# Every other expert's rows: transposed by VectorE from gathered quarters instead of by TensorE

## The chip, the cores and the metric

The kernel runs on one core of a Trainium2 chip. The metric is the device time of one execution in microseconds (us); a time given for a kernel is the median of several runs.

## What is computed

One transformer block: attention over 2048 tokens of width 512, then a mixture of 64 experts (each token goes to 4 of them) plus two shared experts. All data are float32. What matters here is the routed part of the second half:

```python
flat = x.reshape(N, Dx)                    # N = 2048 tokens, Dx = 512
scores = softmax(flat @ Wr + router_bias)  # E = 64 experts
topk_scores, topk_idx = top_k(scores, 4)
...
xb = zeros((E, CAP, Dx)).at[eid, pos].set(flat[tok], mode='drop')   # CAP = 128 seats an expert
h = silu(einsum('ecd,edh->ech', xb, Wg)) * einsum('ecd,edh->ech', xb, Wu)
yb = einsum('ech,ehd->ecd', h, Wd)
y = yb[eid, minimum(pos, CAP - 1)] * (w * valid)[:, None]
out = zeros((N, Dx)).at[tok].add(y)        # and the shared experts are added
```

## The kernel before

The kernel has four stages one after the other, and in each the order of the instructions on every engine is written out by hand.

**Attention** (to about 1772 us from the span's start) goes over heads; its probabilities are brought into 32x32 blocks by DMAs and turned by VectorE (`turn_blocks`, L461).

**Routing and output projection** (1772 to 1968): for each of 16 tiles of 128 tokens, TensorE multiplies the attention outputs by `wo` (L917). The outputs of two tiles (a pair) come from DRAM by `load_ab` (L544) on SP's queue, into one of two buffers `v`. VectorE normalises the tile (`norm`, L728) into `h`, and GpSimd's queue writes `h` to the DRAM tensor `h2d` (L743). TensorE transposes `h` into `h2T` (`turn_h`), computes router logits, and VectorE chooses experts (`choose`, `positions`). `seat_tokens` (L852) adds up, on TensorE, a table of which token sits on which seat of which expert; for the last block VectorE turns the table into token numbers `tok` (128 seats x 64 experts, L869).

**Experts** (2005 to 2371). The steps of expert e are

- `load_xb(e)` (L1190): an indirect DMA on GpSimd's queue gathers the expert's 128 rows of 512 numbers from `h2d` into `xb` (three buffers);
- `expert_turn(e)` (L1199): four 128x128 transposes on TensorE into PSUM (`tpx`, L1202), one copy by ScalarE into `xbT` (L1204);
- `expert_up(e)` (L1206): four matmuls into `pse`, of which there is one PSUM buffer (tag `pl`, `bufs=1`); then `glu`: a sigmoid on ScalarE (L968) and two products on VectorE (L969, L970), of which the last writes `he` and so frees `pse`;
- `expert_mid(e)` (L1222): one transpose `tph` and a copy;
- `expert_down(e)` (L1228): the matmul `psy` (L1230), its product `y` with the gate on VectorE (L1232), and the write to the DRAM tensor `ybd` from ScalarE's queue.

`expert_step(e)` lists, with a cost each, the turn of e+1 (and the gather for e+3), the up of e, the mid of e-1 and the down of e-2. `merge` (L83) lays this list and the list of the shared experts' work beside each other: it always takes the next entry of the list of which the smaller share of cost is done. The shared experts' work comes as units of "pst" products (`first` to `fourth`, L1064; `second` has three additions and three sums of weights on VectorE) and as chains of eight matmuls "psd" (L1126).

**Tail** (from 2371): GpSimd gathers four rows of `ybd` per token (`gather`, L1258), VectorE adds them up, and the last shared work runs on TensorE.

Of the kernel before, what the change touches and what calls it, by code (L numbers as in the profile page):

```python
# [9 lines left out]
F32 = mybir.dt.float32  # L10
BF16 = mybir.dt.bfloat16
U32 = mybir.dt.uint32
AF = mybir.ActivationFunctionType
ALU = mybir.AluOpType
# [4 lines left out]
P = 128  # L19
# [4 lines left out]
def adaln_block_kernel(  # L24
# [23 lines left out]
    nc = tc.nc  # L48
    _, N, D = x.shape
    H, _, DH = Q_w.shape  # L50
    E, _, HE = Wg.shape
    S, _, HS = Sg.shape
    K = 4
    CAP = 128
    NT = N // P
    DC = D // P
# [9 lines left out]
    dram = ctx.enter_context(tc.tile_pool(name="dram", bufs=1, space=DRAM))  # L66

    ident = const.tile([P, P], F32)
# [9 lines left out]
    gb = const.tile([P, D], F32)  # L78
    atd = dram.tile([H, DH, N], F32)
    h2d = dram.tile([N, D], F32)  # L80
    ybd = dram.tile([E * CAP, D], F32)

    def merge(streams, marks):  # L83
# [40 lines left out]
    with ExitStack() as att:  # L124
# [63 lines left out]
        with tc.tile_pool(name="pre", bufs=1) as pre, tc.manual_schedule():  # L188
# [4 lines left out]
            for b in range(NB):  # L193
                xb = pre.tile([P, 4, D], F32, name="xb", bufs=NB)
                nc.sync.dma_start(
                    out=xb, in_=x[0, b * 512 : (b + 1) * 512, :].rearrange("(i p) d -> p i d", p=P)
                )
                xs.append(xb)
                if b == 0:
                    wms = {}  # L200
                    for i in (1, 0):
                        wms[i] = pre.tile([P, DC, D], F32, name="wm", bufs=2)
                        nc.sync.dma_start(
                            out=wms[i],
                            in_=wmod[:, i * D : (i + 1) * D].rearrange("(k p) n -> p k n", p=P),
# [343 lines left out]
        xts = {}  # L549
# [52 lines left out]
        with tc.manual_schedule():  # L602
# [9 lines left out]
            for n, (hd, s) in enumerate(steps):  # L612
# [12 lines left out]
                if hd == H - 1 and s == 0:  # L625
# [4 lines left out]
                    for i in range(0, H, 4):  # L630
                        nc.gpsimd.dma_start(
                            out=wo[:, i : i + 4, :], in_=O_w[i : i + 4].rearrange("h p d -> p h d")
# [39 lines left out]
    keep = ctx.enter_context(tc.tile_pool(name="keep", bufs=1))  # L672
# [8 lines left out]
    psO = ctx.enter_context(tc.tile_pool(name="psO", bufs=2, space=PSUM))  # L681
# [5 lines left out]
    rt = rts.enter_context(tc.tile_pool(name="rt", bufs=1))  # L687
# [4 lines left out]
    iota = rt.tile([P, E], F32)  # L692
    places = rt.tile([P, CAP], F32)
    own = rt.tile([P, 1], F32)
    tok = keep.tile([CAP, E], U32)
    hs_ = {}
    mvs = {}
    logits = {}
# [5 lines left out]
    def route_consts():  # L704
        nc.sync.dma_start(out=wr, in_=Wr.rearrange("(k p) e -> p k e", p=P))
        nc.sync.dma_start(out=rb, in_=router_bias.partition_broadcast(P))
        make_upper_triangular(nc, before, val=1.0, diag=False)
        nc.gpsimd.memset(onesb, 1.0)
        nc.gpsimd.iota(
            iota, pattern=[[1, E]], base=0, channel_multiplier=0,  # L710
            allow_small_or_imprecise_dtypes=True,
        )
        nc.gpsimd.iota(
            places, pattern=[[1, CAP]], base=0, channel_multiplier=0,
            allow_small_or_imprecise_dtypes=True,
        )
        nc.gpsimd.iota(
            own, pattern=[[0, 1]], base=0, channel_multiplier=1,
            allow_small_or_imprecise_dtypes=True,
        )  # L720

    def load_x(j):
        nc.sync.dma_start(
            out=acc[:, 4 * j : 4 * j + 4, :],
            in_=x[0, j * 512 : (j + 1) * 512, :].rearrange("(i p) d -> p i d", p=P),
        )

    def norm(t):  # L728

        st = rt.tile([P, 6], F32, name="st", bufs=3)  # L730
        nc.vector.bn_stats(st, acc[:, t, :])
        mv = rt.tile([P, 2], F32, name="mv", bufs=3)
        nc.vector.bn_aggr(mv, st)
        rstd = rt.tile([P, 1], F32, name="rstd", bufs=3)
        nc.scalar.activation(rstd, mv[:, 1:2], AF.Sqrt, bias=eps, scale=1.0)
        nc.vector.reciprocal(rstd, rstd)
        h = rt.tile([P, D], F32, name="h", bufs=4)
        nc.vector.tensor_scalar(
            h, acc[:, t, :], mv[:, 0:1], rstd, ALU.subtract, ALU.mult
        )  # L740
        nc.vector.tensor_mul(h, h, cb)
        nc.vector.tensor_add(h, h, sb)
        nc.gpsimd.dma_start(out=h2d[t * P : (t + 1) * P, :], in_=h)  # L743
        hs_[t] = h

    def turn_h(t):
# [105 lines left out]
    def seat_tokens(b):  # L852


        t0, nt = BLOCKS[b]
        seat, who = seats.pop(b)
        for n in range(nt * K):
            i, k = divmod(n, K)
            nc.tensor.matmul(
                out=table,  # L860
                lhsT=seat[:, n, :],
                rhs=who[:, i, k].rearrange("p j e -> p (j e)"),
                start=(b == 0 and n == 0),
                stop=(b == len(BLOCKS) - 1 and n == nt * K - 1),
            )
        if b == len(BLOCKS) - 1:
            tb = rt.tile([CAP, 2 * E], F32, name="tb")
            nc.vector.tensor_copy(tb, table)
            nc.vector.scalar_tensor_tensor(  # L869
                tok, tb[:, E:], float(P), tb[:, :E], ALU.mult, ALU.add  # L870
            )

    table = psO.tile([CAP, 2 * E], F32, name="table", tag="tr")
    ALL = ((0, 4), (4, 8), (8, 12), (12, 16))
# [12 lines left out]
    with tc.manual_schedule():  # L887
# [6 lines left out]
        for t in range(NE):  # L894
            ps = psO.tile([P, D], F32, name="pso", tag="y")
            nc.tensor.matmul(
                out=ps,
                lhsT=last3[:, t * P : (t + 1) * P] if t < NE - 1 else ones,
                rhs=wo[:, H - 1, :],
                start=True,  # L900
                stop=True,
# [4 lines left out]
        for t in range(NE, NT):  # L906
# [3 lines left out]
            if i == 1 and pr >= NP - 1 - S:  # L910
                s = pr - (NP - 1 - S)
# [3 lines left out]
            ps = psO.tile([P, D], F32, name="pso", tag="y")  # L915
            for hd in range(H):
                nc.tensor.matmul(  # L917
                    out=ps,
                    lhsT=abs_[pr][:, hd, i * P : (i + 1) * P],
                    rhs=wo[:, hd, :],  # L920
                    start=(hd == 0),
                    stop=(hd == H - 1),
# [20 lines left out]
    with ExitStack() as ex:  # L943
# [11 lines left out]
        def load_up(e):  # L955
            w = ewp.tile([P, DC, 2, HE], F32, name="wgu")
            nc.sync.dma_start(out=w[:, :, 0, :], in_=Wg[e].rearrange("(k p) h -> p k h", p=P))
            nc.sync.dma_start(out=w[:, :, 1, :], in_=Wu[e].rearrange("(k p) h -> p k h", p=P))
            weights[e] = w
# [5 lines left out]
        def glu(dst, pg, pu, width):  # L965

            sig = sgp.tile([P, width], F32, name=f"sig{width}")
            nc.scalar.activation(sig, pg, AF.Sigmoid)  # L968
            nc.vector.tensor_mul(sig, sig, pg)  # L969
            nc.vector.tensor_mul(dst, sig, pu)  # L970
# [213 lines left out]
        xbp = wts.enter_context(tc.tile_pool(name="xbp", bufs=2))  # L1184
        xbs = {}
        xts = {}
        ups = {}
        hts = {}

        def load_xb(e):  # L1190
            xbs[e] = xbp.tile([CAP, D], F32, name="xb", bufs=3)
            nc.gpsimd.indirect_dma_start(  # L1192
                out=xbs[e][:, :],
                out_offset=None,
                in_=h2d[:, :],
                in_offset=bass.IndirectOffsetOnAxis(ap=tok[:, e : e + 1], axis=0),
            )

        def expert_turn(e):  # L1199
            tp = psO.tile([P, DC, P], F32, name="tpx", tag="tr")  # L1200
            for k in range(DC):
                nc.tensor.transpose(tp[:, k, :], xbs[e][:, k * P : (k + 1) * P], ident)  # L1202
            xts[e] = xbp.tile([P, DC, CAP], F32, name="xbT")
            nc.scalar.copy(xts[e], tp)  # L1204

        def expert_up(e):  # L1206
            ps = psO.tile([P, 2 * HE], F32, name="pse", tag="pl", bufs=1)
            for k in range(DC):
                nc.tensor.matmul(  # L1209
                    out=ps,  # L1210
                    lhsT=xts[e][:, k, :],
                    rhs=weights[e][:, k].rearrange("p i h -> p (i h)"),
                    start=(k == 0),
                    stop=(k == DC - 1),
                )
            if e + 3 < E:
                load_up(e + 3)
            he = xbp.tile([CAP, HE], F32, name="he")
            glu(he, ps[:, :HE], ps[:, HE:], HE)
            ups[e] = he  # L1220
# [7 lines left out]
        def expert_down(e):  # L1228
            ps = psO.tile([CAP, D], F32, name="psy", tag="y")
            nc.tensor.matmul(out=ps, lhsT=hts[e], rhs=downs[e], start=True, stop=True)  # L1230
            y = xbp.tile([CAP, D], F32, name="y")
            nc.vector.tensor_mul(y, ps, gb)  # L1232
            nc.scalar.dma_start(out=ybd[e * CAP : (e + 1) * CAP, :], in_=y)

        def expert_step(e):
            out = []

            def turn():
                if e + 3 < E:
                    load_xb(e + 3)  # L1240
                expert_turn(e + 1)

            def down():
                expert_down(e - 2)
                if e + 1 < E:
                    load_down(e + 1)

            if e + 1 < E:
                out.append((512, turn))
            if e < E:  # L1250
                out.append((1024, lambda: expert_up(e)))
            if 0 <= e - 1 < E:
                out.append((128, lambda: expert_mid(e - 1)))
            if e >= 2:
                out.append((512, down))
            return out
# [34 lines left out]
        with tc.manual_schedule():  # L1291
# [13 lines left out]
            for n, (_, f) in enumerate(tail):  # L1305
                f()
                upto = min(NT, READY[n])
                while done < upto:
                    t = order[done]
# [37 lines left out]
```

## Time and profile before

| | |
|---|---|
| median of 3 runs | 2510.37 us (2509.43 to 2513.41) |
| the profiled execution | 2493.62 us, its span 2491.8 us |
| mean granted TensorE clock | 0.994 of full speed |
| TensorE busy | 2419.3 us, 97% of the span |
| VectorE busy | 1514.8 us, 61% |
| DMA traffic | 326.25 MB in 224399 packets |
| transposes `tpx` (L1202) | 256, mean 273 ns |
| copies `xbT` (L1204) | 64, mean 585 ns |
| gathers `xb` (L1192) | 64, mean 1012 ns on GpSimd's queue |
| GpSimd's queue in the expert stage | waits 269.8 us in 58 waits for TensorE's `tpx` |

PE is TensorE, PEld its loading of weights, DVE VectorE, ACT ScalarE, POOL GpSimd, SP the queue that only issues DMAs; a small q (SPq, ACTq) marks an engine's DMA issues. Matmuls overlap on TensorE, so the duration of one is longer than the distance from its start to the next one's. A row of a group gives: line, engine, operation, what it writes and reads, count, then total busy time and mean of one in ns, then how long the engine was idle before them and what ended that. A row of the timeline gives start, length, engine, line and operation; brackets hold the idle time before it.

### The profile page before, as it was taken

Reading aid. Unit: us, or ns where it says so; the run is one execution under the profiler, and the core shown is the slowest. Engines: PE = TensorE matmul, PEld = TensorE weight load, DVE = VectorE, ACT = ScalarE, POOL = GpSimd, SP = SyncE. Lnnn points to the kernel's source line nnn. Section 1 sums busy time; section 2 is a strip of 40 time slices with the busy share of each in tenths; the row PEclk is TensorE's granted clock in tenths of the full one; section 3 lists DMA queues with packets and bytes.
Section 4 is the critical chain, followed back from the end, with each engine's and each line's share of the span. In section 5 each row is a group of like instructions: output and inputs, shape, how many; then the busy total and the mean of one; then the engine's idle time right before and its main releaser. Section 6 shows DMA issues by size and latency. Waiting matters only on the chain.

```text
span 2491.8 us, 26256 instructions
## 1 busy us (share of the span) xinstructions
PE 2419.3 (97%) x8525; PEld 1526.6 (61%) x8525; DVE 1514.8 (61%) x2966; ACT 656.0 (26%) x1476; POOL 249.2 (10%) x314
## 2 busy tenths in 40 slices
PE   7999999999999999999999999979999999999999
PEld 4666666666666666666666666545554476876844
DVE  4566666666666666666666666565465572553664
ACT  3233233332333323333233333221111221222200
POOL 0000000000000000000000000041000021111164
PEclk9999999999999999999999999989999999999999
DMA  4234434444344443444444444475524266878665
GB/s 140 62 91 107 116 95 110 107 103 109 90 121 102 97 120 94 112 111 103 109 97 121 104 101 108 109 227 135 164 81 152 89 180 209 250 213 251 198 191 161
DMA packets 224399, 326.25 MB, mean 131 GB/s; under 512 B 32100, under 2 KB 140680, under 8 KB 224264
## 3 DMA queue, kind: packets, MB, share of 16 engines
q1 hardware_dynamic: 195656, 246.96, 38.4%
q0 software_dynamic: 19392, 60.84, 8.1%
q10 hardware_dynamic: 9216, 16.78, 1.8%
q8 instruction: 69, 1.13, 0.2%
q14 instruction: 66, 0.54, 0.1%
HBM read 139.91 MB, written 41.94 MB: 73 GB/s over the span
## 4 chain that ended last, share of the span: by engine, by line
PE 67%; DVE 17%; SPq 6%; DMA 4%; issue 4%; ACT 1%; DVEq 0%; POOL 0%; ACTq 0%; POOLq 0%
PE pqk L169 12%; PE ps L408 12%; PE po L479 9%; DVE pt L461 7%; PE pso L917 6%; SPq L451 6%; PE pv L329 5%; PE pst L1064 5%; PE pse L1209 4%; PE psd L1126 4%; DVE nm L421 4%; DMA pt<-p 3%; PE psg L980 3%; DVE p L397 3%; PE psy L1230 2%
## 5 line engine op out<-in xcount | busy, mean ns | idle before, releaser
L427 ACT ACTIVATE p<-ps,nm 128x1024 f32<-128x1024 f32 (+7 forms) x384 | 331.9, 864 | 1040.5 <-DVE nm L425 368.4
L408 PE MATMUL ps<-kt,qt 128*128 128x512 f32 (+3 forms) x1280 | 535.2, 535 | 43.0 <-ACT p L427 42.1
L479 PE MATMUL po<-pt,v 128*128 128x256 f32 (+1 forms) x2304 | 567.5, 369 | 7.0 <-DVE pt L461 3.6
L479 PEld LDWEIGHTS po<-pt,v 128*128 128x128 f32 x2304 | 426.4, 191 | 220.3 <-issue 155.8
L421 DVE TENSOR_REDUCE nm<-ps 128x1 f32<-128x1024 f32 (+7 forms) x384 | 349.6, 910 | 91.1 <-PE ps L408 82.4
L461 DVE STREAM_TRANSPOSE pt<-pt 128x1664 f32<-128x1664 f32 (+2 forms) x160 | 318.0, 1988 | 64.2 <-DMA pt<-p 59.9
L408 PEld LDWEIGHTS ps<-kt,qt 128*128 128x128 f32 x1280 | 235.5, 191 | 193.3 <-issue 126.9
L420 DVE TENSOR_TENSOR ps<-ps,causal 128x128 f32<-128x128 f32 x256 | 74.4, 291 | 349.9 <-PE ps L408 349.9
L489 POOL DMA_DIRECT2D atd<-at x128 | 78.2, 612 | 1650.0 <-ACT at L488 1625.4
L329 PE MATMUL pv<-wv,hT 128*128 128x256 f32 x1024 | 240.4, 379 | 0.0
L169 PE MATMUL pqk<-hT,wk 128*128 128x512 f32 x512 | 232.7, 598 | 0.0
L169 PE MATMUL pqk<-hT,wq 128*128 128x512 f32 x512 | 231.4, 596 | 0.0
L397 DVE TENSOR_SCALAR p<-p,rs 128x1024 f32<-128x1024 f32 (+7 forms) x384 | 221.7, 606 | 9.3 <-DMA p<-atd 0.2
L329 PEld LDWEIGHTS pv<-wv,hT 128*128 128x128 f32 x1024 | 195.0, 190 | 31.0 <-issue 1.9
L917 PE MATMUL pso<-hT,v 128*128 128x512 f32 x384 | 173.7, 598 | 0.0
L169 PEld LDWEIGHTS pqk<-hT,wk 128*128 128x128 f32 x512 | 98.3, 193 | 102.9 <-issue 100.5
L169 PEld LDWEIGHTS pqk<-hT,wq 128*128 128x128 f32 x512 | 98.1, 192 | 97.1 <-issue 93.9
L1209 PE MATMUL pse<-wgu,xbT 128*128 128x256 f32 x512 | 121.1, 380 | 0.0
L917 PEld LDWEIGHTS pso<-hT,v 128*128 128x128 f32 x384 | 69.7, 191 | 71.4 <-issue 70.4
L1126 PE MATMUL psd<-wsd,hs 128*128 128x512 f32 x256 | 111.5, 593 | 0.0
L1209 PEld LDWEIGHTS pse<-wgu,xbT 128*128 128x128 f32 x512 | 93.9, 191 | 11.6 <-issue 1.0
L1192 POOL DMA_INDIRECT xb<-h2d,tok x64 | 64.8, 1012 | 300.8 <-PE tpx L1202 269.8
(264 smaller groups left out, 1943.3 us busy)
## 6 DMA issues: line engine op xcount, KB each, us to landing
pt<-p SPq DMA_DIRECT2D x768, 104.0 KB, 2.2
pt<-p SPq DMA_DIRECT2D x256, 124.0 KB, 2.3
pt<-p SPq DMA_DIRECT2D x256, 108.0 KB, 2.2
atd<-at POOLq DMA_DIRECT2D x128, 128.0 KB, 2.3
wgu<-in_L_ffn_Wg_dram SPq DMA_DIRECT2D x64, 256.0 KB, 4.3
wgu<-in_L_ffn_Wu_dram SPq DMA_DIRECT2D x64, 256.0 KB, 4.7
wd<-in_L_ffn_Wd_dram SPq DMA_DIRECT2D x64, 256.0 KB, 3.9
ybd<-y ACTq DMA_DIRECT2D x64, 256.0 KB, 3.7
```

Of the source, the lines that this page charges most:

```text
L169: nc.tensor.matmul(out=ps, lhsT=w[:, k, :], rhs=hT[:, k, j * 512 : (j + 1) * 512], start=(k == 0), stop=(k == DC - 1),)
L329: nc.tensor.matmul(out=ps, lhsT=hT[:, k, t * P : (t + 1) * P], rhs=wv[:, k].rearrange("p i d -> p (i d)"), start=(k == 0), stop=(k == DC - 1),
L397: nc.vector.tensor_scalar(cols[:, :, a:b], cols[:, :, a:b], rs[:, n : n + 1], None, ALU.mult)
L408: nc.tensor.matmul(out=ps[:, o : o + wo], lhsT=q, rhs=kts[hd, (c0 + o) // 512][:, :wo], start=True, stop=True,)
L421: nc.vector.tensor_reduce(nm[:, n : n + 1], ps[:, :w], AX.X, ALU.max, negate=True)
L427: nc.scalar.activation(rows[:, r0 + c0 // P : r0 + (c0 + w) // P], ps[:, :w].rearrange("q (r b k) -> q r b k", b=4, k=32), AF.Exp, bias=nm ...
L451: nc.sync.dma_start(out=pt[32 * b : 32 * (b + 1), a * w : (a + 1) * w], in_=pb[32 * a : 32 * (a + 1), b * w : (b + 1) * w],)
L461: nc.vector.transpose(part, part)
L479: nc.tensor.matmul(out=po if wide else po[:, P:], lhsT=vts[g][:, kt, hh * DH : (hh + 1) * DH], rhs=rows[:, r : r + last + 1 : last] if wid ...
L917: nc.tensor.matmul(out=ps, lhsT=abs_[pr][:, hd, i * P : (i + 1) * P], rhs=wo[:, hd, :], start=(hd == 0), stop=(hd == H - 1),)
L1126: nc.tensor.matmul(out=ps, lhsT=hsh[b, f][:, i * P : (i + 1) * P], rhs=wsd[:, f, :], start=(f == 0), stop=(f == NHC - 1),)
L1209: nc.tensor.matmul(out=ps, lhsT=xts[e][:, k, :], rhs=weights[e][:, k].rearrange("p i h -> p (i h)"), start=(k == 0), stop=(k == DC - 1),)
```

## The change

- `norm` also writes each tile of `h`, in four DMAs on SP's queue, to a second DRAM tensor `h2q`. There a token's row is four quarters of 128 numbers; quarter b holds columns 32b to 32b+31 of each of the four chunks of 128 columns.
- After the last seats, four small matmuls with slices of the identity (`pick`, made by GpSimd in `route_consts`) spread the token numbers so that partition 32a+r has, for b = 0 to 3, the token of seat 32b+r; VectorE makes 4 x token + a of it (`tokq`).
- For odd experts `load_xb` gathers with four indirect DMAs of 128 rows of 128 numbers from `h2q`. The tile then consists of 32x32 blocks that already lie in the block that they belong to after a transpose.
- For odd experts `expert_turn` is one VectorE instruction that transposes the sixteen 32x32 blocks of each group of 32 partitions, straight into `xbT`; TensorE's four transposes and ScalarE's copy remain for even experts.
- In `expert_step` the turn of an odd expert counts 0 in place of 512, which shifts how `merge` lays the two lists beside each other.

```diff
+    h2q = dram.tile([N, D], F32)
...
+    quarter = rt.tile([P, 1], F32)
+    pick = rt.tile([P, 4, 4, 32], F32)
     tok = keep.tile([CAP, E], U32)
+    tokq = keep.tile([P, 4, E], U32)
...
+        for b in range(4):
+            nc.gpsimd.memset(quarter[32 * b : 32 * (b + 1), :], float(b))
+            nc.gpsimd.tensor_copy(pick[:, :, b, :], ident.rearrange("p (t r) -> p t r", r=32))
...
         nc.gpsimd.dma_start(out=h2d[t * P : (t + 1) * P, :], in_=h)
+        for b in range(4):
+            nc.sync.dma_start(
+                out=h2q[t * P : (t + 1) * P, b * P : (b + 1) * P].rearrange(
+                    "p (k d) -> p k d", d=32
+                ),
+                in_=h.rearrange("p (k b d) -> p b k d", b=4, d=32)[:, b],
+            )
...
             nc.vector.scalar_tensor_tensor(
-                tok, tb[:, E:], float(P), tb[:, :E], ALU.mult, ALU.add
+                tb[:, :E], tb[:, E:], float(P), tb[:, :E], ALU.mult, ALU.add
             )
+            nc.vector.tensor_copy(tok, tb[:, :E])
+            ps = psO.tile([P, 4, E], F32, name="psq", tag="tr")
+            for b in range(4):
+                nc.tensor.matmul(
+                    out=ps[:, b, :],
+                    lhsT=pick[:, b].rearrange("p a r -> p (a r)"),
+                    rhs=tb[:, :E],
+                    start=True,
+                    stop=True,
+                )
+            nc.vector.tensor_scalar(tokq, ps, 4.0, quarter, ALU.mult, ALU.add)
...
         def load_xb(e):
...
+            else:
+                xbs[e] = xbp.tile([P, D], F32, name="xb", bufs=3)
+                for b in range(4):
+                    nc.gpsimd.indirect_dma_start(
+                        out=xbs[e][:, b * P : (b + 1) * P],
+                        out_offset=None,
+                        in_=h2q.rearrange("n (b f) -> (n b) f", b=4),
+                        in_offset=bass.IndirectOffsetOnAxis(ap=tokq[:, b, e : e + 1], axis=0),
+                    )
...
         def expert_turn(e):
...
+            else:
+                xt = xbp.tile([P, DC, CAP], F32, name="xbT")
+                nc.vector.transpose(
+                    xt.rearrange("p k (b s) -> p b k s", s=32),
+                    xbs[e].rearrange("p (b k s) -> p b k s", b=4, s=32),
+                )
+                xts[e] = [xt[:, k, :] for k in range(DC)]
...
             if e + 1 < E:
-                out.append((512, turn))
+                out.append((512 if e % 2 == 1 else 0, turn))
```

More of the change, by code (lines that the diff above doesn't have):

```diff
@@ L1190, in load_xb @@
         def load_xb(e):
[L1191 to L1197, printed above, removed]
-        def expert_turn(e):
[L1200 to L1204, printed above, removed]
+            if e % 2 == 0:
+                xbs[e] = xbp.tile([CAP, D], F32, name="xb", bufs=3)
+                nc.gpsimd.indirect_dma_start(
+                    out=xbs[e][:, :],
+                    out_offset=None,
+                    in_=h2d[:, :],
+                    in_offset=bass.IndirectOffsetOnAxis(ap=tok[:, e : e + 1], axis=0),
+                )
+            else:
+                xbs[e] = xbp.tile([P, D], F32, name="xb", bufs=3)
+                for b in range(4):
+                    nc.gpsimd.indirect_dma_start(
+                        out=xbs[e][:, b * P : (b + 1) * P],
+                        out_offset=None,
+                        in_=h2q.rearrange("n (b f) -> (n b) f", b=4),
+                        in_offset=bass.IndirectOffsetOnAxis(ap=tokq[:, b, e : e + 1], axis=0),
+                    )
+        def expert_turn(e):
+            if e % 2 == 0:
+                tp = psO.tile([P, DC, P], F32, name="tpx", tag="tr")
+                for k in range(DC):
+                    nc.tensor.transpose(tp[:, k, :], xbs[e][:, k * P : (k + 1) * P], ident)
+                xt = xbp.tile([P, DC, CAP], F32, name="xbT")
+                nc.scalar.copy(xt, tp)
+                xts[e] = [xt[:, k, :] for k in range(DC)]
+            else:
+                xt = xbp.tile([P, DC, CAP], F32, name="xbT")
+                nc.vector.transpose(
+                    xt.rearrange("p k (b s) -> p b k s", s=32),
+                    xbs[e].rearrange("p (b k s) -> p b k s", b=4, s=32),
+                )
+                xts[e] = [xt[:, k, :] for k in range(DC)]
         def expert_up(e):
@@ L1210, in expert_up @@
                     out=ps,
-                    lhsT=xts[e][:, k, :],
+                    lhsT=xts[e][k],
                     rhs=weights[e][:, k].rearrange("p i h -> p (i h)"),
```

## The prediction

> **What bounds the kernel now.** The first view is the busy table with the 40 slices: TensorE is busy 97% of the span and nine tenths or more in all slices but two. VectorE, second, is at 61%.
>
> ```profile
> PE 2419.3 (97%) x8525; PEld 1526.6 (61%) x8525; DVE 1514.8 (61%) x2966; ACT 656.0 (26%) x1476; POOL 249.2 (10%) x314
> ...
> PE   7999999999999999999999999979999999999999
> ```
>
> Second, the same by stretches: the routing stage (1805 to 1968 us from the span's start), the whole expert stage (2005 to 2371), and inside it a part with "pst" units (2125 to 2230) and one with "psd" chains (2060 to 2125). The columns are engine busy times, clock, DMA share and GB/s.
>
> ```profile
> 2125.00:2230.00 105.00, 105.00 (x495) 85.06 (x495) 66.74 (x162) 27.00 (x71) 20.80 (x19) 1.00 0.81 240
> 2060.00:2125.00 65.00, 65.00 (x245) 40.58 (x244) 17.99 (x41) 12.60 (x36) 10.39 (x11) 1.00 0.72 217
> 2005.00:2371.00 366.00, 366.00 (x1599) 272.39 (x1598) 189.00 (x448) 84.00 (x228) 61.70 (x62) 1.00 0.74 222
> 1805.00:1968.00 163.00, 162.69 (x560) 81.64 (x559) 95.27 (x266) 23.96 (x37) 5.40 (x10) 1.00 0.27 94
> ```
>
> TensorE is full through all 366 us of the expert stage, at the full granted clock; VectorE is 52% busy there (64% among units), GpSimd 17%, the DMA engines 74%. Third, the list of waits from 2006 us on, TensorE's own rows: one wait of 0.7 us. So here TensorE's work sets the end, and a microsecond taken from its queue is a microsecond, as long as nothing new makes it wait.
>
> **What is removed.** 32 of 64 `expert_turn` lose four transposes on TensorE and a PSUM copy on ScalarE. Two rows by form give durations, and the timeline of one step gives what a step costs:
>
> ```profile
> L1202 PE MATMUL tpx<-ident,xb 128*128 128x128 f32 x256 | 38.2, 273 | 0.0
> L1204 ACT COPY xbT<-tpx 128x512 f32<-128x512 f32 x64 | 37.3, 585 | 145.9 <-DVE y L1232 58.0 <-PE tpx L1202 33.9 <-PE pse L1209 22.2
> ```
>
> ```profile
> 2086.75 0.60 PE L1202 MATMUL tpx<-ident,xb 128*128 128x128 f32 x4
> ...
> 2087.18 1.89 PE L1209 MATMUL pse<-wgu,xbT 128*128 128x256 f32 x8
> ...
> 2088.91 0.27 PE L1224 MATMUL tph<-ident,he 128*128 128x128 f32 x1
> ...
> 2089.02 1.02 PE L1230 MATMUL psy<-wd,heT 128*128 128x512 f32 x2
> 2089.11 0.28 ACT L968 ACTIVATE sig<-pse 128x128 f32<-128x128 f32 x1 [0.43 <-PE pse L1209]
> ...
> 2089.75 0.29 DVE L970 TENSOR_TENSOR he<-sig,pse 128x128 f32<-128x128 f32 x1
> ...
> 2089.88 0.60 PE L1202 MATMUL tpx<-ident,xb 128*128 128x128 f32 x4
> ```
>
> Read starts, not durations: the transposes overlap, and from the first one's start to the next matmul's is 2087.18 - 2086.75 = 0.43 us (0.44 a step later). So 32 x 0.435 = **13.9 us** leave TensorE's queue. The ScalarE copies (32 x 0.585) lie beside it and bring nothing. "TensorE: Matmul & The Clock Gate", Part 4, in the Trainium skill, gives a transpose about 275 ns in a kernel, which agrees with the mean of 273 ns here; as a price it would make 128 x 0.275 = 35 us, an estimate from that page. The spacing of the starts decides against it.
>
> **What is added, beside other work.**
> (a) VectorE: 32 block transposes, 128x512. Line L461 has three widths: 1664 in 1.907 us, 1984 in 2.238, so 1.03 ns a column and 0.19 fixed: 0.72 us each, 23 us in 366. The nearest rows bound it: a 128x512 scalar pass takes 0.547 (L738), the 1664 form 1.91; the four-dimensional pattern is not in the trace, and I take 0.72. Units then go from 64% to about 70%. I charge 0.5 us of new waits; the range keeps 0 to 6.
> (b) GpSimd: an odd expert needs four gathers. An unblocked gather starts every 1.25 us (2002.71, 2004.13 at the stage's start: 1.42), so a pair of experts costs 5 x 1.3 = 6.5 us of the 11.1 that it lasts (355 us / 64 x 2). `load_xb(e+3)` is released by the turn of e and needed at the turn of e+3, three steps on, at least 14.6 us in the new order. Four gathers take 3 x 1.3 to the last start, and 4.8 us (median of xb's landing, 8.4 at most) to land: 8.7, or 12.3 at worst. Cost nothing; without that cover VectorE stands in its queue, and the sigmoid products behind it hold `pse`.
> (c) SP: 64 writes to `h2q`, four a tile, 512 pieces of 128 bytes each; nearest `wr`, 512 pieces of 256 bytes, issued in 0.44 us and landed in 7.2 behind other loads. SP waits for `h` of the tile; what is queued behind are the next pair's `load_ab` (L544) and the shared weights. `h` of the last tile of a pair is ready 7 to 8 us after the pair's last matmul (h2d issues at 1814.79 and 1846.97; pairs end at 1807.5 and 1839), four issues take 2.4, the loads 2 and land in 5.2: 18 us into a pair that lasts 31.7. So 13 us of slack; TensorE waits for nothing. The DMA engines are 27% busy there. Last, `wgu` now follows tile 15's writes: 1979 in place of 1969, ten us of issue, landed by about 1995, wanted after 2008. Cost 0, kept 0 to 4. "DMA: Bandwidth & Descriptors", Specifications, speaks against this edit: pieces under 512 bytes cost a read-modify-write. If that doubled these writes, the 13 us would still hold them; no row here shows 128-byte pieces.
> (d) `pick` and `quarter`, eight small GpSimd operations after 1773.3, ahead of the first h2d write at 1780.5 (0.16 to 0.3 us are rows like them). They hide.
>
> **What is added on the path.**
> (e) The four `psq` matmuls stand in TensorE's queue right after the seat table and need `tb`. Now `tb` is written 1999.77 to 2000.05, the token indices end at 2000.32, and TensorE went on at 1999.41. Hand-over 0.2, then four 128x64 products of two passes (L758: eight starts in 0.84): TensorE goes on at 2001.4. **+2.0 us** (1.5 to 2.5).
> (f) In the new order the first `pse` follows expert 0's transposes at once; before, expert 1's and two products stood between. The copy is exposed: transposes at 2012.39, copy at 2013.08 for 0.58, 0.2 to hand over, less the 0.43 of the transposes: **+1.0** (0.8 to 1.3).
> (g) Expert 2's gather waits behind expert 1's four: POOL starts at about 2002.4, expert 2's gather at 2009, landing near 2013.7; TensorE wants it at 2013.4. **+0.5** (0 to 3).
> (h) `pse` has one buffer. In the step above, `pse` ends at 2088.91 and is free at 2090.04 (end of `he`), plus 0.2: 1.33 us. Between two `pse` stand tph 0.11, psy 0.87 and the transposes 0.43: 1.41, just enough. An odd step with nothing of the shared expert in it now has 0.98: wait 0.35. The changed order has eight such steps (11, 13, 17, 19, 41, 43, 45, 49): **+2.8** (0 to 3.5).
>
> **Sum:** -13.9 + 2.0 + 1.0 + 0.5 + 2.8 + 0.5 = **-7.1 us**. The profiled execution took 2493.62 (span 2491.8); it would be 2486.5. It lies 16.8 us under the median of the runs, 2510.37; nothing in the trace says where that is, and I take the step off the median: **2503.3**. What follows the expert stage (gathers of `ybd`, psd chains) begins from its last expert and moves up whole. A difference of 0.2%, 5 us, is about what a measurement of this kernel tells from none.
>
> **Rivals.**
> 1. *The covers are better than I charge*: (h) and (a) vanish, -13.9 + 3.5 = -10.4, 2500. For: at (h) TensorE has waited for nothing so far. Against: the arithmetic of one `pse` buffer. Chance 0.15.
> 2. *VectorE's queue takes it back.* The transposes stand ahead of the sigmoid products; among units VectorE also has 2.5 us of sums in one piece. Were each odd step late by 0.3 us, 32 x 0.3 = 9.6 more: +2, 2513; at half of that -2, 2508. For: in-order queue, 70%. Against: no TensorE wait for VectorE beyond 0.7 us today, and the tight steps hold few sums. Chance 0.25, about no change.
> 3. *Slower: the four gathers come too late.* Place: `load_xb` on POOL in the short stretches. It decides once issue and landing exceed 14.6 us: with 1.3 a gather the landing must pass 10.7 us (8.4 is the longest now), or a gather must cost 2.2 us in place of 1.3, so that five fill a pair. At 1 us late per odd expert: -7 + 32 = +25, 2535; at half, +9, 2519. For: DMA already at 81% among units, and the quarters are four times as many pieces of a quarter the size. Against: the bytes are the same, and the weights already come in 512-byte rows at 4.3 to 4.7 us. Chance 0.2, the routing stage's delays (c) included.
> 4. *It does not do what it says*: half the transposes still on TensorE. The order of instructions shows 32 groups of four in place of 64, so no weight.
>
> **Numbers.** Forecast 0.40 (2499 to 2507), rival 1 0.15, rival 2 0.25 (2506 to 2514), rival 3 0.20 (2515 and up, half of it under 2521). The range 2496 to 2520 leaves out the upper half of rival 3 and a little below. Faster by over 0.2%: 0.55; within: 0.25; slower: 0.20.
>
> **What would show it.** Right: the expert stage some 10 us shorter and TensorE still full; 128 tpx in place of 256; a stop of 1 us before psq and of 0.35 us before `pse` in the eight steps, ended by `he`; L1249 near 0.72 us; no TensorE wait on `v`. Wrong: VectorE idle before L1249 until a DMA of `xb` in many steps (rival 3), `pse` held by a late `sig` (rival 2), or TensorE waiting for `v<-atd` in the routing stage.

## The result, and the profile after

In the first comparison the changed kernel took 2509.65 us (2504.44 to 2516.13, 12 runs), the kernel before 2510.51 (2508.22 to 2513.75, 12 runs): ratio 0.9995, 95% interval 0.9986 to 1.0004. That is no difference that can be measured; the forecast was 7.1 us less. The profiled execution took 2504.44 us (span 2502.4), where 2486.5 was worked out.

One thing has to be said ahead of the rest. The later runs came to several chips, and these are of two sorts: on some the kernel before takes about 2497 us, on the others about 2510. The first comparison was made where it takes 2510; the profile of before that the prediction stands on (2493.62) has the time of the 2497 sort; like all profiles of that sort it holds landing times of gathers, which no profile of the 2510 sort does. Below, "a 2497 chip" and "a 2510 chip" mean just that, and every ratio is against runs of before on the same chip.

The page of the changed kernel, then the stretches of the prediction (columns: busy time of TensorE, weight load, VectorE, ScalarE and GpSimd, clock, DMA share, GB/s):

```profile
PE 2414.9 (97%) x8405; PEld 1514.2 (61%) x8405; DVE 1534.0 (61%) x3000; ACT 637.0 (25%) x1443; POOL 342.9 (14%) x418
...
PE   7999999999999999999999999979999989999989
```

```profile
1805.00:1968.00 163.00, 161.88 (x551) 80.46 (x550) 96.44 (x272) 23.96 (x37) 5.40 (x10) 1.00 0.39 111
2005.00:2371.00 366.00, 357.32 (x1470) 259.95 (x1469) 208.18 (x481) 65.79 (x196) 154.02 (x158) 0.99 0.73 221
2060.00:2125.00 65.00, 64.41 (x229) 39.30 (x228) 25.44 (x56) 8.65 (x28) 24.97 (x27) 1.00 0.74 224
2125.00:2230.00 105.00, 104.80 (x475) 83.97 (x474) 74.03 (x175) 22.72 (x65) 48.32 (x50) 1.00 0.80 245
```

TensorE is no longer full: 8.7 us are missing in the expert stage, of which only 0.8 lie in the two inner stretches and 7.1 ahead of 2060 us. What was to be taken away and added is there, with the durations that were worked out (groups by form):

```profile
L1249 DVE STREAM_TRANSPOSE xbT<-xb 128x512 f32<-128x512 f32 x32 | 22.4, 701 | 2.0 <-DMA xb<-h2q,tokq 2.0
L1243 PE MATMUL tpx<-ident,xb 128*128 128x128 f32 x128 | 19.3, 273 | 0.0
L1245 ACT COPY xbT<-tpx 128x512 f32<-128x512 f32 x32 | 18.7, 583 | 63.4 <-PE tpx L1243 21.2 <-DVE y L1281 18.9 <-PE pst L1092 11.6
```

What is new and was not foreseen stands at the top of TensorE's waits (us in total, times, longest):

```profile
PE psg L1008 <- DVE acc L1322: 7.9, 1, 7.9
PE pse L1258 <- ACT heT L1275: 6.3, 1, 6.3
```

The 6.3 us in the timeline, first TensorE, then ScalarE, VectorE and GpSimd:

```profile
2014.14 1.89 PE L1258 MATMUL pse<-wgu,xbT 128*128 128x256 f32 x8
2015.87 0.27 PE L1273 MATMUL tph<-ident,he 128*128 128x128 f32 x1
2015.98 1.03 PE L1092 MATMUL pst<-silc,wsu 128*128 128x256 f32 x4
2016.85 1.03 PE L1092 MATMUL pst<-h2T,ws 128*128 128x256 f32 x4
2024.18 3.75 PE L1258 MATMUL pse<-wgu,xbT 128*128 128x256 f32 x8 [6.31 <-ACT heT L1275]
```

```profile
2023.06 0.28 ACT L996 ACTIVATE sig<-pse 128x128 f32<-128x128 f32 x1 [8.60 <-remote]
```

```profile
2020.89 0.42 DVE L1112 TENSOR_TENSOR v<-u,pst 128x256 f32<-128x256 f32 x1 [7.98 <-issue]
```

```profile
2018.39 0.95 POOL L1232 DMA_INDIRECT xb<-h2q,tokq  x1 [0.30 <-issue]
2019.65 0.95 POOL L1232 DMA_INDIRECT xb<-h2q,tokq  x1 [0.30 <-issue]
2025.86 0.95 POOL L1223 DMA_INDIRECT xb<-h2d,tok  x1 [5.26 <-DVE xbT L1249]
```

Read them across. The second `pse` is done at about 2016.0, but ScalarE, which wants nothing else, starts its sigmoid at 2023.06; VectorE gets the `pst` product that it waits for at 2020.89, too. By the ends that the profile gives (for matmuls they are modelled), TensorE's results were there, and the others learnt of them some 7 us late. TensorE then waits in turn, because the one `pse` buffer is free only when `he` is written, at 2023.97 (the view names `heT`, which ended at about the same time). After the wait its `pse` takes 3.75 us in place of 1.89: half clock. And GpSimd had issued 15 gathers without a pause, 1.25 us apart, from 2001.7 on; the last ends at 2020.60, and 0.3 us later VectorE goes on. The second wait, at 2422, comes at the end of a run of 36 gathers (2375.7 to 2423.4), too.

### The profile page after: what moved, and what is told of

Same layout as the page of the kernel before. It is cut to its first block, busy times and chain, and to the rows that moved or that the text cites. A ratio compares the mean times of both kernels' runs of the same rounds, so it can differ in the third digit from the quotient of the medians.

```text
span 2502.4 us, 26290 instructions
## 1 busy us (share of the span) xinstructions
PE 2414.9 (97%) x8405; PEld 1514.2 (61%) x8405; DVE 1534.0 (61%) x3000; ACT 637.0 (25%) x1443; POOL 342.9 (14%) x418
## 4 chain that ended last, share of the span: by engine, by line
PE 67%; DVE 17%; SPq 6%; issue 4%; DMA 4%; ACT 1%; DVEq 0%; ACTq 0%; POOL 0%; POOLq 0%
PE pqk L172 12%; PE ps L411 12%; PE po L482 9%; DVE pt L464 7%; SPq L454 6%; PE pv L332 5%; PE pso L945 5%; PE pse L1258 5%; PE pst L1092 4%; PE psd L1154 4%; DVE nm L424 4%; PE psg L1008 4%; DMA pt<-p 3%; DVE p L400 3%; PE psy L1279 2%
## 5 line engine op out<-in xcount | busy, mean ns | idle before, releaser
L1232 POOL DMA_INDIRECT xb<-h2q,tokq x128 | 126.0, 985 | 96.9 <-PE tpx L1243 66.1
```

## Ledger of three stretches

All that follows is read with one ledger, from start times of TensorE in each profile: "front" from the first router product `pl` to the first `tpx`, "stage" from there to the last `pst`, "tail" to the last `psd`.

| profile (us) | chip | front | stage | tail |
|---|---|---|---|---|
| before, the one predicted from | not listed | 216.91 | 370.22 | 110.65 |
| before_again | 2497 | 216.90 | 370.23 | 111.87 |
| after_again | 2497 | 216.73 | 361.13 | 111.80 |
| before_third | 2510 | 216.91 | 370.22 | 124.92 |
| after_third | 2510 | 216.80 | 370.22 | 125.67 |
| after, first comparison | 2510 | 216.79 | 370.08 | 120.73 |

On a 2497 chip the change takes 9.1 us out of the stage. On a 2510 chip it takes nothing out of it; and there the tail is 9 to 14 us longer, for both kernels.

## The experiments

**before_again**: the kernel before, nothing changed.

> A second profiled execution of the kernel before, nothing changed. The first took 2493.62 us and lies 17 us under all its timed runs; it shows no stretch of half clock after 1692 us and no TensorE wait over 0.75 us after 2006. Theory A (the lost gain is the change's own doing: the small pieces and the quarter gathers make TensorE stall at 2017 and 2422): this profile again shows neither, and any extra time lies before 1700 us. Theory B (stalls of 6 to 8 us with half clock behind them come to both kernels, and the first profile of before happened to lack them): a typical execution, 2505 to 2513, shows one or more of them after 2000 us here too.

Measured: 2494.5 us, on a chip where 15 runs of before have a median of 2497.54. No TensorE wait over 1.1 us after 2000. It decides nothing between the two theories, since the typical execution on this chip is another than in the first comparison; that the chips differ was first seen here.

**removal_only** (same chip): the transposes are left out, nothing is added.

```
         def expert_turn(e):
+            if e % 2 == 1:
+                xts[e] = xts[e - 1]
+                return
...
-                out.append((512, turn))
+                out.append((512 if e % 2 == 1 else 0, turn))
```

> Kernel before, with the transposes and the copy of every odd expert left out: odd experts multiply the tokens of the expert before them, so the output is not the reference's. The order of the steps is that of the changed kernel; nothing is added. By the sum of the prediction: -13.9 for the transposes, +1.0 for the exposed first copy, +2.8 for the one pse buffer, so about -10 us, 2500. Theory C (TensorE's time is paid back whatever is removed, by half clock or by other waits): within 3 us of before. Theory A: at least -9, and no stall of over 3 us after 2006.

Measured: 2488.44, ratio 0.9958 (0.9945 to 0.9972), 9 to 10 us less. Theory C falls: what is taken from TensorE's queue is gained.

**vector_only** (same chip): VectorE transposes, one gather an expert.

```
-                nc.scalar.copy(xts[e], tp)
+            if e % 2 == 0:
...
+            else:
+                nc.vector.transpose(
+                    xt.rearrange("p k (b s) -> p b k s", s=32),
+                    xbs[e].rearrange("p (b k s) -> p b k s", b=4, s=32),
+                )
```

> Kernel before, with the odd experts' rows gathered in one piece as before and transposed in 32x32 blocks on VectorE; the blocks are left out of place, so odd experts compute with wrong columns. No h2q, no psq, no quarter gathers. By the sum: -13.9 + 1.0 + 2.8 + 0.5 = -9.6, 2501. If VectorE's queue takes the gain back (rival 2): -4 to +2. Its difference to the run that only removes is the price of the VectorE transposes.

Measured: 2487.16, ratio 0.9962 (0.9948 to 0.9975). Its stage is 360.72 us, removal_only's 360.72 too. The 32 VectorE transposes cost nothing.

**front_only** (same chip): `h2q`, `pick`, `psq` and `tokq` added, `load_xb` and `expert_turn` as before.

> Kernel before, with the added work ahead of the expert stage alone: the h2q writes, pick, quarter, the four psq products and tokq. All experts are gathered and turned as before. By the sum: +2.0 for psq and nothing else, 2512.5. Theory A in its first form (512 pieces of 128 bytes a write hold something up): +5 or more, with TensorE waiting for v between 1800 and 1970 or with late weights after 2000.

Measured: 2495.38, ratio 0.9996 (0.9987 to 1.0005); front 216.72, stage 370.23. Nothing, where +2 was expected. The 2.0 us are there (the last table product starts at 1999.71, the next shared product 2.0 later), but one wait of TensorE for `h` has shrunk, from 3.0 us in before to 0.7: the shared-expert products stand otherwise among the tiles (the first `psg` at 1898.6 in before_again, at 1933.3 here). Why they stand otherwise is open.

**after_again**: the changed kernel, on another 2497 chip.

> The changed kernel once more, nothing altered. So far the parts add up to a gain: the run without transposes and the one with VectorE transposes lie 9 to 10 us under before, and the added work ahead of the stage costs nothing that can be measured. If the parts simply add, the changed kernel is 8 to 10 us under before here. Theory A2 (the quarter gathers, the one part not yet tried alone, take it back): within 3 us of before, with TensorE waits of 6 us or more near 2017 and 2422 again and half clock behind them. Theory B2 (the two waits belong to that one execution): the profile shows none.

Measured: 2487.32, ratio 0.9963 (0.9952 to 0.9975), 9 to 10 us less, and its profiled execution 2486.25, for which 2486.5 was worked out. Theory A2 falls on this chip. TensorE's waits from 1690 us on are the ones that the prediction named:

```profile
PE pse L1258 <- PE psy L1279: 1.6, 8, 0.2
PE tp L766 <- DVE h L752: 1.1, 2, 0.7
PE psg L1008 <- DVE u L1116: 0.9, 1, 0.9
PE psq L892 <- DVE tb L886: 0.9, 1, 0.9
PE pse L1258 <- ACT xbT L1245: 0.8, 1, 0.8
...
PE tpx L1243 <- DMA xb<-h2d,tok: 0.2, 1, 0.2
```

The view counts from the modelled end of a matmul. From start to start, as the prediction counts, each of the eight costs 0.36:

```profile
2071.92 1.02 PE L1279 MATMUL psy<-wd,heT 128*128 128x512 f32 x2
2073.14 1.97 PE L1258 MATMUL pse<-wgu,xbT 128*128 128x256 f32 x8 [0.20 <-PE psy L1279]
```

Two `psy` take 0.86, so `pse` could start at 2072.78 and starts at 2073.14.

**gathers_only** (same chip as after_again): four gathers for odd experts, into natural order, all turned on TensorE.

```
+                for q in range(4):
+                    nc.gpsimd.indirect_dma_start(
+                        out=xbs[e][:, q * P : (q + 1) * P],
...
+                        in_=h2d.rearrange("n (q f) -> (n q) f", q=4),
```

> Kernel before with one thing altered: the odd experts' rows come by four indirect gathers of 512-byte quarters in place of one of 2 KB rows, into the same place, so that all is still turned on TensorE and the output is the reference's. Theory A2: 6 to 14 us over before, with a TensorE wait of some 6 us early in the expert stage. If the gathers hide as the prediction had it: 0, at most +2 for the first expert's later start.

Measured: 2501.51, ratio 1.0017 (1.0008 to 1.0025), 4 us more: neither of the two. The profile's stage is 376.4, 6.2 more, and all of it is at the start, where expert 1 is wanted right behind expert 0 and its quarters land one by one:

```profile
2007.74 0.71 PE L1215 MATMUL tpx<-ident,xb 128*128 128x128 f32 x5
2009.41 0.33 PE L1215 MATMUL tpx<-ident,xb 128*128 128x128 f32 x1 [0.95 <-DMA xb<-h2d,tokn]
2010.47 0.33 PE L1215 MATMUL tpx<-ident,xb 128*128 128x128 f32 x1 [0.73 <-DMA xb<-h2d,tokn]
2011.85 0.48 PE L1215 MATMUL tpx<-ident,xb 128*128 128x128 f32 x1 [1.06 <-DMA xb<-h2d,tokn]
2012.12 1.92 PE L1068 MATMUL pst<-h2T,wsg 128*128 128x256 f32 x4
```

From start to start the waits cost 3.35 us, and the half clock behind them 2.8 more (four `pst` in 1.7 us in place of 0.86). After 2018 the quarters cost nothing. In the changed kernel expert 1 goes to VectorE and nobody stands behind these gathers but VectorE, for 2.0 us.

**order_only** (same chip): before with the new costs of the turn.

> Kernel before with only the cost of the even steps' turn in the hand-made order set to 0, as in the changed kernel; all the work is as before. Expected 0 by every theory, within 2 us; where it differs, the new order itself has a price, for which the prediction charged only the exposed copy (+1.0).

Measured: 2500.01, ratio 1.0008 (0.9999 to 1.0017). Stage 370.85, 0.6 more: the exposed copy. The interval reaches from nothing to 4 us more, so this can't be told from what was expected.

**start_fix**, on a 2510 chip, as the next three: the changed kernel with expert 1 on TensorE with one gather, `psq` one shared product later.

```
+                if n == 8:
+                    quarters()
...
+            return e == 1 or e % 2 == 0
```

> The changed kernel with two of its prices taken away: expert 1 is gathered in one piece and turned on TensorE (so its transposes stand between expert 0's and the first pse, and the first four gathers are single), and the psq products stand one psg half later in TensorE's queue, when tb is long written. Where the changed kernel has 0.89 us of wait before psq and 0.80 before the first pse, this one has neither, and pays 0.43 for expert 1's transposes: 1 to 1.5 us under the changed kernel, which the times can hardly tell; the trace must show both waits gone. If it is not so, the two waits were hiding something that now shows.

Measured: 2506.61 (2497.26 to 2517.95), ratio 0.9988 (0.9976 to 0.9999). The waits before `psq` and the first `pse` are gone, but in their place TensorE waits 2.3 us for the first `tpx`: the first gather came later. In one_of_four, which has the same start, `tokq` ends at 2002.43 and the first gather starts at 2003.37; in after_again 2000.50 and 2001.43, so both times 0.9 us behind `tokq`, with the wait put down to VectorE. `psq` seems to stand on the way to the first gather, too, and not only in TensorE's queue; moving it later doesn't pay. More telling is the stage: 362.9 us against 370.2 for the changed kernel on the same chip. GpSimd's first long run is 9 gathers here (with one pause of 0.6 us) in place of 15, and of the stall of 6 us there are left two waits of 1.4 and 1.0; 31 of the 32 VectorE transposes and the other quarters are still there. This reading has a limit: the profiled execution is the fastest of the twelve, 2497.26, 9.3 us under their median. A typical one may stop for longer.

**three_of_four** (same chip): 46 experts on VectorE. The lines that differ from start_fix:

```
-            return e == 1 or e % 2 == 0
+            return e < 3 or e % 4 == 0
```

> As the run with the mended start, but experts 0 to 2 and then every fourth are turned on TensorE, the other 46 in quarters on VectorE. By the sum: 46 x 0.435 = 20.0 us leave TensorE's queue in place of 13.9, 1.3 us of start waits go, and each further bare step waits 0.2 before pse (1 to 2 us in all): some 5 to 6 us under the changed kernel, 15 under before. GpSimd then issues 13 gathers for four experts, 16.3 of 21.5 us. If the gathers come too late (rival 3 of the prediction): VectorE idle before its transpose until a DMA of xb, in many steps, and no gain or a loss against the changed kernel.

Measured: 2548.24, ratio 1.0142 (1.0124 to 1.0160), 36 to 38 us more. The stage alone is 409.2. The three largest of TensorE's waits from 2006 to 2420 us:

```profile
PE pse L1269 <- issue: 22.1, 9, 4.9
PE pse L1269 <- ACT heT L1286: 7.9, 2, 4.6
PE psy L1290 <- ACT heT L1286: 5.0, 3, 1.9
```

VectorE waits for no DMA of `xb` anywhere in the stage, and never idles 0.2 us before one of its 46 transposes, so the gathers are not late: rival 3 would have shown that. The weights are not late either: at all seven stops of TensorE in the stage (2.9 us or more from one start to the next) `pse` begins 0.1 to 0.2 us after VectorE has written `he` of the expert before, which is what frees its buffer. What GpSimd has is eight runs of 12 gathers, with no pause over 0.4 us. Six of the seven stops end within 9 us after the end of such a run; behind the other two runs TensorE stops for 2.0 and 2.2 us; the seventh stop (3.0 us, at 2041) follows shorter runs. This kernel ran on no 2497 chip. One of the six, TensorE, then ScalarE, then GpSimd:

```profile
2061.23 1.12 PE L1290 MATMUL psy<-wd,heT 128*128 128x512 f32 x2 [1.30 <-ACT heT L1286]
2066.86 3.75 PE L1269 MATMUL pse<-wgu,xbT 128*128 128x256 f32 x8 [4.50 <-issue]
```

```profile
2060.64 0.37 ACT L1108 COPY p<-pst 128x256 f32<-128x256 f32 x1 [5.36 <-PE tph L1284]
```

```profile
2056.51 0.95 POOL L1243 DMA_INDIRECT xb<-h2q,tokq  x1 [0.30 <-issue]
2057.76 0.95 POOL L1243 DMA_INDIRECT xb<-h2q,tokq  x1 [0.30 <-issue]
2066.53 0.95 POOL L1234 DMA_INDIRECT xb<-h2d,tok  x1 [7.81 <-DVE sig L1003]
```

The run of gathers ends at 2058.71, and ScalarE gets its `pst`, five microseconds after it began to wait, at 2060.64.

**after_third** (same chip): the changed kernel.

> The changed kernel again. On the chip of the run before it lay 0.37% under before, while in the first comparison, on a chip on which both kernels took 13 us or more longer, it gained nothing and its profile held two TensorE waits of 6.3 and 7.9 us with half clock behind them. Theory D (the two waits belong to the chip, not to the kernel): a chip where before takes about 2497 gives 0.996 and none of the waits; a chip where before takes about 2510 gives 0.999 to 1.000 and shows them again. Theory E (chance of the single execution): the ratio does not go with the time of before.

Measured: 2510.13 (10 runs), before 2510.44: ratio 0.9999 (0.9990 to 1.0008). Theory D holds: the wait of 6.0 us in the expert stage and one of 6.3 in the tail are back.

```profile
PE psg L1008 <- DVE sig L997: 6.3, 1, 6.3
PE pse L1258 <- ACT heT L1275: 6.0, 1, 6.0
PE psg L1008 <- issue: 4.0, 3, 2.1
```

**before_third** (same chip): the kernel before.

> The kernel before once more, for its profile on this chip. Theory D: where before takes about 2510, its profile shows waits of several us with half clock behind them too, after 2000 us or ahead of it; where it takes about 2497, none.

Measured: 2511.3 us. TensorE's only wait after 2006 us, and VectorE's beside it (the latter from 2380 to 2445):

```profile
PE psg L980 <- issue: 12.7, 1, 12.7
```

```profile
DVE sig L969 <- issue: 10.0, 1, 10.0
DVE acc L1133 <- remote: 8.6, 1, 8.6
```

So the stall of the tail belongs to both kernels on such a chip. It lies within 44 unbroken gathers of `yg` (2379.1 to 2437.8), without a quarter gather or a VectorE transpose in the stretch. The expert stage of before, where GpSimd issues one gather and pauses, has none.

**one_of_four**, on another 2510 chip: experts 3, 7, ..., 63 on VectorE, the start as in start_fix. The lines that differ from three_of_four:

```
-            return e < 3 or e % 4 == 0
+            return e < 3 or e % 4 != 3
```

> The changed kernel with the mended start and with only every fourth expert (3, 7, ..., 63: sixteen) gathered in quarters and transposed by VectorE. By the sum 16 x 0.435 = 7.0 us leave TensorE's queue, no start wait is paid, and 7 gathers serve four experts in place of 10: 5 to 7 us under before on any chip. Theory F (on the slower kind of chip, TensorE's late releases come from how closely GpSimd's gathers follow each other): 5 to 7 under before there too, with no TensorE wait over 2 us between 2006 and 2370. Theory G (they come with the quarters whatever their number): little or nothing gained on such a chip.

Measured: 2506.54, ratio 0.9987 (0.9978 to 0.9996), 3 to 4 us less than before; some 2 us short of theory F's sum. Its sign holds, and its trace but for one wait over 2 us, the 2.3 before the first `tpx`, which start_fix has, too. TensorE's waits in the stage:

```profile
PE tpx L1254 <- issue: 2.3, 1, 2.3
PE pse L1269 <- PE psy L1290: 0.8, 4, 0.2
```

Stage 365.53, so 4.7 less than before: 16 x 0.435 = 7.0, less 2.3 that come back mostly before `pse` in bare steps. The front is 1.3 longer, with the 2.3 us before the first `tpx` in it. After 2016 GpSimd has no unbroken run of more than five gathers until the tail.

## Why the prediction was right and wrong

**The terms**, on the 2497 chip of after_again, start to start on TensorE:

- Transposes: 32 x 0.435 = 13.9 gone, as said.
- (a) VectorE 0.70 us each (0.72 said); the charge of 0.5 was not paid, since vector_only and removal_only have the same stage.
- (c) and (d) 0 said: front_only's ratio is 0.9996 (0.9987 to 1.0005), and the `h2q` writes, of which the prediction had no like row, land there in 2.5 us (median; 10.7 at most).
- (e) +2.0 said. From the last table product to the next shared one it is 2.02 in place of 0.06; but the shorter wait for `h` gave it back (front 216.73 in place of 216.90), which no step had.
- (f) +1.0 said, 0.96. (g) +0.5 said, 0.34.
- (h) 0.35 in eight steps said, 0.36 in eight steps, 2.9 in all, and 0.6 more inside these `pse` groups.

The stage: -13.9 + 0.96 + 0.34 + 2.9 + 0.6 = -9.1, and 361.13 - 370.23 = -9.1. The forecast for these terms was -13.9 + 1.0 + 0.5 + 2.8 + 0.5 = -9.1. Ratio and interval there put the gain at 6 to 12 us; 7.1 was forecast. That the sum came out at 2486.5 against 2486.25 for one execution is partly luck: executions on that chip spread by 7 us, and the 2.0 of (e) was in the sum but not in the time. On the chip of the first comparison, 2509.65 lies inside the stated range, 2496 to 2520, but outside the forecast's own 2499 to 2507: there the range held and the mechanism didn't.

**The step that failed** is "I take the step off the median". The 16.8 us between the profiled execution and the median, of which the text says that nothing in the trace tells where they are, were taken for a constant that the change would leave alone. Some 13 of them belong to the chip (the medians of before are 2510.4 and 2497.5), and the rest lies within the spread of the runs on one chip. Where they are can be seen by comparing before_third with before_again, two executions that are 16.8 us apart, too: front and stage are the same to 0.02 us and the tail is 13.1 longer, with the 12.7 us stall and half clock; the remaining 3.8 lie ahead of the routing stage. And what makes that stall does not leave the change alone.

**The other step** is (b), "Cost nothing". Its arithmetic held everywhere (1.25 us between gathers; no wait of VectorE for `xb` but 2.0 us once, and no lateness of gathers even at 13 for four experts). On a 2510 chip the cost came by a way that (b) didn't weigh: not gathers that arrive late, but TensorE's results that the others see late while GpSimd issues without a pause. There the stage loses 6.5 us of wait and some 2.5 of half clock, which is the whole gain.

**Rivals.** The outcome of the first comparison is the time of rival 2 (about no change), but not its mechanism: VectorE's queue takes nothing back. Rival 3 has the right place, the four gathers on GpSimd, and with three of four its sign, but not its cause.

**Shown, and open.** Shown is that, in the expert stage of a 2510 chip, the stall goes with the length of GpSimd's runs. Pauses after each gather (before) and runs of at most five after the start (one_of_four) give none; one run of 15 gives one of 6 us, in both profiles; with 9 in that run, 1.4 and 1.0 us are left, in that one execution; of eight runs of 12, six have a stall at their end.

The lateness itself can be read apart from TensorE's waits: from the end of an expert's last `pse` product to the start of its `sig`, for all 64 experts of a profile. In the profile predicted from and in all seven of 2497 chips it is never over 1.02 us, within runs of 9 and 20 gathers, too (a pause under 0.65 us counted as none). On the 2510 chips the latest `sig` whose product ends within a run is 7.0 and 6.8 us late in the two runs of 15, 3.1 to 6.2 in seven of the eight runs of 12, 2.1 to 4.4 in eight of the eleven runs of 9, 3.0 in one of four runs of 8, and 1.5 at most in runs of six or fewer; in three_of_four some products end just outside a run, with a `sig` up to 2.9 late. TensorE mostly does not feel the runs of 9, since other work covers them, as here in after_third (a run from 2095.6 to 2106.7), where `sig` is 2.2 us late and TensorE goes on with `psd`:

```profile
2101.47 1.89 PE L1258 MATMUL pse<-wgu,xbT 128*128 128x256 f32 x8
2103.19 4.03 PE L1154 MATMUL psd<-wsd,hs 128*128 128x512 f32 x9
```

```profile
2105.59 0.28 ACT L996 ACTIVATE sig<-pse 128x128 f32<-128x128 f32 x1 [2.63 <-remote]
```

So neither VectorE's transposes nor quarter gathers as such are enough: in the changed kernel both go on all through the stage in runs of four and five, with nothing over 0.7 us late. And in the tail of before, gathers without either are enough. But the length of a run does not settle the size: in start_fix's profile 62 gathers of `yg` without a pause stop TensorE for 3.4 us at most from start to start, where 44 in before_third stop it for 13.3.

Not tried on a 2510 chip: quarter gathers alone, and VectorE's transposes alone; both ran on 2497 chips only. Open is what differs between the chips, and by what way gathers hold up the others' knowledge of TensorE's results. Instruction loads don't tell: a load of TensorE's instructions lies at 2407.7 in the tail of before_again and at 2411.0 in before_third, and takes 0.96 and 0.99 us. The records can't settle it, either: on the 2510 chips the trace lacks the landing times of DMAs and, in the changed kernel, 71 and 82 of TensorE's 1364 signals, so that only the engines that wait show the lateness. Late signals and lost records come on the same chips; whether the recording has a part in the lateness no run shows.

**Better than both?** On a 2497 chip the changed kernel itself is the fastest of those that compute the whole block (0.9963). On a 2510 chip one_of_four and start_fix gain 0.13 and 0.12%, both with intervals just under 1. The changed kernel with its first gathers spread out, so that no run is longer than five, was not tried.

## What to carry to other kernels

Before taking a sum from one profile to a median, ask whether that execution belongs to the runs: 16 us below the lowest of them said that it did not, and the answer was worth more than any of the added terms. Count TensorE from start to start and a sum over edits can close to 0.1 us; the price of an added wait is read as well as that of a removed product. And an engine at 40% may still do harm by how it spends it: of GpSimd's gathers look not only at share and landing, but at the longest run without a pause.

## What was not expected of the hardware

- On a 2510 chip, engines that wait for TensorE stand idle up to 10 us within long runs of indirect gathers 1.25 to 1.35 us apart (2001.7 to 2020.6 in the stage, 2379 to 2438 in the tail); on a 2497 chip 64 such gathers in one run (2368.6 to 2455.1 in after_again) leave no stall of TensorE over 1 us.
- After a wait of 6.3 us TensorE's products come at half speed for some 5 us: `pse` in 3.75 us in place of 1.89. Three waits of 0.95, 0.73 and 1.06 did the same in gathers_only, where TensorE had only eight transposes in 4.4 us (2007.74 to 2012.12); the clock from 2012 to 2016 is 0.50. A single wait of 3.0 us (for `h`, at 1972) did it in some executions only: the clock from 1960 to 2006 is 1.00 in before_again and 0.93 in removal_only, with the same 3 us idle in both (before_again first):

```profile
1960.00:2006.00 46.00, 43.02 (x138) 20.56 (x137) 27.92 (x70) 10.08 (x14) 4.22 (x5) 1.00 0.39 122
```

```profile
1960.00:2006.00 46.00, 43.02 (x135) 20.74 (x133) 27.44 (x71) 9.59 (x13) 2.04 (x3) 0.93 0.35 109
```

  By the Trainium skill, "TensorE: Matmul & The Clock Gate", Part 1, the clock is halved after an idle window of some 3.4 us that runs freely. The wait of 6.3 us agrees with it; that of 3.0 has only four transposes behind it (0.46 us) and so comes to about a window's length, which may or may not fill one; that the transposes count as idle there, and among the three short waits, no run here shows. The half clock is worth 3 us, the front of removal_only being 219.9 where before_again's is 216.9, and may be part of the spread of the runs.
- A 128x512 float32 transpose in 32x32 blocks with a four-dimensional pattern takes VectorE 0.70 us, as the plain ones of line L461 would at that width.
